# A graph-attention layer on one core: output rows made between the loop's steps instead of after the loop

## The chip, the cores and the metric

The kernel runs on one core of a Trainium2 chip. The metric is the device time of one execution in microseconds (us). Seventeen executions of the kernel before were timed; a further one was recorded by the hardware profiler, and all rows shown here are from that one.

## What is computed

12,500 nodes with 128 features, 212,500 edges sorted by their target `dst`. Cut to what matters:

```
h   = relu(layernorm(x))
q, v = h @ Wq.T + bq, h @ Wv.T + bv          # per node, 8 heads of 16
k   = edge_attr @ Wk.T + bk                  # per edge
in_m, out_m, diag_m = sum(q[src]*k), sum(q[dst]*k), sum(q[src]*q[dst])   # per edge and head
score = (softmax of each of the three over the edges of a node, summed) * edge_weight**lam
out = x + leaky_relu(segment_sum(score * v[dst]) @ Wo.T + bo)
```

Since `v[dst]` is the same for all edges of a node, a node needs from its edges only two sums for each of 24 softmaxes (3 kinds by 8 heads): the denominator and the weighted numerator.

## The kernel before

`ordered_path` relies on the order of `dst`, and sets a flag if a property that it needs does not hold. After it `general_path` runs if the flag is set; with the inputs of the reference it is not.

**Preparation.** x is loaded, the statistics `inv` and `shift` of the layer norm are taken, and q is computed and written to `q_table` in DRAM (`nodes_q`, L808 and L809), then again as three bf16 terms to `q3_table` (`terms_q`, L821 to L830). Two tables `sums` in DRAM, 48 numbers for each node, are filled with zeros from `blank` (L864, 28 DMAs on SyncE's queue, two behind each of the first `q_table` writes).

**The loop.** The edges lie in S = 5 parts that are worked in parallel, each of T = 84 blocks of 512 edges (the last block of a part is also the first of the next, but for the fifth). A *step* t takes block t of all five parts; an *iteration* g = 5 t + s takes one block. What an iteration does:

- `gather(g + 9)`: four indirect DMAs (L608), issued by GpSimd (POOL), fetch q of the sources. The ring `qq` has 11 buffers, so a gather for g + 9 waits for `logits(g - 2)`.
- `project(g + 1)`, `turn(g + 2)`, `spread_q(g + 2)`: TensorE (PE) transposes the edge features, multiplies them by Wk into `k_ps` (2 buffers), and picks q of the targets; ScalarE (ACT) copies the results.
- `logits(g)`: VectorE (DVE) multiplies q by q (L968), both by k (L969), and sums over each head (L971).
- Once a step, spread over its five iterations, the scans of the step before: `turn_logits` (s = 0), `scan_max` (s = 1, DVE), `to_rows` (PE) and `powers` (ACT) (s = 2), `scan_sums` (s = 3, DVE), `select` (s = 4, DVE). `put_rows(t - 2)` at s = 4 writes the finished sums of up to 42 nodes of each part to DRAM (L1074, 5 DMAs on SyncE's queue), at a node index that is read from the data; even parts go to one table, odd parts to the other.

The small PSUM tiles of the scans (`small`) share one ring of three buffers. The order on each engine is the program's order, which `pin` fixes: every pinned instruction comes after the one pinned before it on its engine. SyncE's queue (SP) carries `fetch_edges(g + 6)` (ring `ea` of 7), `fetch(t + 2)` at s = 3 and `put_rows`, in that order.

**The last stage.** When all sums are written, a loop over 7 chunks of 7 units (a unit is 256 nodes, 49 in all) loads the sums of both tables (`ab`) and x again, adds the tables, divides, and for every four tiles of 128 nodes: relu (L1145), transpose (L1152), copy, product with Wv (L1158), times the score (L1160), transpose (L1167), copy, product with Wo (L1173), copy, leaky relu (L1176), add x (L1178), store.

Of the kernel before, what the change touches and what calls it, by code (L numbers as in the profile page):

```python
# [7 lines left out]
F32 = mybir.dt.float32  # L8
# [8 lines left out]
HEADS = 8  # L17
# [455 lines left out]
def ordered_path(ctx: ExitStack, tc: tile.TileContext, flag, x, src, dst, edge_attr, edge_weight,  # L473
# [14 lines left out]

    nc = tc.nc
    N, F = x.shape
    E = src.shape[0]
# [16 lines left out]
    R = S * H3  # L510
    NU, CU = NI // 2, 7
    CH = 2 * CU
    LAST = N // 2 - (NU - 1) * P
    assert NI % 2 == 0 and NU % CU == 0 and N % 2 == 0 and 96 <= LAST < P

    dram = ctx.enter_context(tc.tile_pool(name="dram", bufs=1, space=DRAM))
    q_table = dram.tile([NP, F], F32, name="q_table")
    q3_table = dram.tile([3 * NP, F], BF, name="q3_table")
    rel_d = dram.tile([NB, BE], BF, name="rel_d")
    fa_d = dram.tile([NB, 4, BE], BF, name="fa_d")  # L520
    sums = [dram.tile([NP, 2 * H3], F32, name=f"sums{i}") for i in range(2)]


    consts = ctx.enter_context(tc.tile_pool(name="consts", bufs=1))
# [34 lines left out]

    inv = consts.tile([P, NI], F32, name="inv")  # L560
    shift = consts.tile([P, NI], F32, name="shift")
    blank = consts.tile([P, CU * 2 * H3], F32, name="blank")
    nc.vector.memset(blank, 0.0)
    src_i = consts.tile([P, NB, JN], I32, name="src_i")
    ends = consts.tile([P, NB, JN], F32, name="ends")
    bases = consts.tile([1, T, 8], I32, name="bases")
    tops = consts.tile([1, T, 8], I32, name="tops")
    LOOK, QQ, AHEAD, EA = 9, 11, 6, 7
    edges = ctx.enter_context(ExitStack())
    gath = edges.enter_context(tc.tile_pool(name="gath", bufs=QQ))  # L570
# [4 lines left out]
    def pin(inst):  # L575

        engine = str(inst.ins.engine)
        if engine in pinned:
            tc.add_manual_dep(inst.ins, pinned[engine], mybir.DependencyInfo(
                mybir.DependencyClass.NoSync, mybir.DependencyReason.DATA), reason="in order")  # L580
        pinned[engine] = inst.ins.name
        return inst
# [31 lines left out]
    def units(t, lo, n, c):  # L614

        return t[lo * 2 * P:(lo + n) * 2 * P, :].rearrange("(u p k) c -> p u (k c)", p=P, k=2)
# [11 lines left out]
    with tc.tile_pool(name="prep", bufs=1) as prep, \  # L628
# [14 lines left out]
        b_row = prep.tile([1, 3, F], F32, name="b_row")  # L643
        for i, b in enumerate((bv, bk, bo)):
            pin(nc.sync.dma_start(b_row[:, i, :], b[None, :]))
        nc.vector.memset(bases, 0)
        nc.vector.memset(tops, 0)
        for s in range(S):
# [204 lines left out]
        for g in range(-2, GN):  # L853
            if g + 2 < GN:
                rectify(g + 2)
            if 0 <= g + 1 < GN:
                turn_h(g + 1)
            if g >= 0:
                nodes_q(g)
            ready(g + 4)  # L860
            measure(g + 6 + min(max(g, 0), 6))
            if 0 <= g < NI // CU:
                for t in sums:
                    pin(nc.sync.dma_start(t.rearrange("(p i) r -> p (i r)", p=P)  # L864
                                          [:, g * CU * 2 * H3:(g + 1) * CU * 2 * H3], blank))
            if g in side:
                side[g]()
        for g in range(LOOK):
# [6 lines left out]
                edges_5()  # L875
        bad = got["bad"]

        found = prep.tile([1, 5], F32, name="found")
        bad_ps = prep_ps.tile([1, P], F32, name="t_ps")
        pin(nc.tensor.transpose(bad_ps[:, :RW], bad, ident[:RW, :RW]))  # L880
        nc.vector.tensor_reduce(found[:, 0:1], bad_ps[:, :RW], AX.X, ALU.min)  # L881
        nc.vector.tensor_scalar(found[:, 0:1], found[:, 0:1], 0.0, None, op0=ALU.is_lt)
        base_f = prep.tile([1, T, 8], F32, name="base_f", tag="terms")
        pin(nc.vector.tensor_copy(base_f, bases))
        top_f = tops.bitcast(F32)
        pin(nc.vector.tensor_copy(top_f, tops))
# [6 lines left out]
        nc.vector.tensor_sub(halo[:, 0:S - 2], base_f[:, 1, 2:S], base_f[:, 0, 1:S - 1])  # L893
        nc.vector.tensor_scalar(halo[:, 0:S - 2], halo[:, 0:S - 2], float(W) - 0.5, None, op0=ALU.is_lt)
        nc.vector.tensor_reduce(found[:, 3:4], halo[:, 0:S - 2], AX.X, ALU.max)
        nc.vector.tensor_reduce(found[:, 4:5], found[:, 0:4], AX.X, ALU.max)
        nc.vector.tensor_copy(flag, found[:, 4:5])


    with tc.tile_pool(name="work", bufs=2) as work, \  # L900
            tc.tile_pool(name="scan", bufs=2) as scan, \
# [76 lines left out]
        def small(shape, name):  # L978
            return ps.tile(shape, F32, name=name, tag="small", bufs=3)
# [90 lines left out]
        def put_rows(t):  # L1070
            for i, (lo, own) in enumerate(trios):
                for k in own:
                    if lo + k == 0 or t > 0:
                        pin(nc.sync.dma_start(sums[(lo + k) % 2][bass.ds(base_v[t][lo + k], W), :],  # L1074
                                              st[t]["rows"][k * W:(k + 1) * W, i, k, :]))
            del st[t], base_v[t]

        def later(f, t):
            if 0 <= t < T:
                f(t)  # L1080

        fetch(0)
        fetch(1)
# [7 lines left out]
        for g in range(end + 2 * S):  # L1091
# [25 lines left out]
            else:  # L1117
                later(select, t - 1)
                later(put_rows, t - 2)

    edges.close()


    with tc.tile_pool(name="fin", bufs=2) as fin, \
            tc.tile_pool(name="fin_ps", bufs=2, space=PSUM) as fin_ps:
        for lo in range(0, NU, CU):
            ab = fin.tile([P, 2, CH, 2 * H3], F32, name="ab", bufs=3)
            for i in range(2):
                nc.sync.dma_start(ab[:, i].rearrange("p (u k) r -> p u (k r)", k=2),
                                  units(sums[i], lo, CU, 2 * H3))  # L1130
            x_in = fin.tile([P, CH, F], F32, name="x_in", bufs=3)
            nodes_in(x_in, lo, CU, nc.sync)
            tot = fin.tile([P, CH, 2, H3], F32, name="tot")
            nc.vector.tensor_add(tot.rearrange("p n i c -> p n (i c)"), ab[:, 0], ab[:, 1])
            ratio = fin.tile([P, CH, H3], F32, name="ratio")
            nc.vector.tensor_scalar(ratio, tot[:, :, 0, :], 1e-30, None, op0=ALU.max)
            nc.vector.reciprocal(ratio, ratio)  # L1137
            nc.vector.tensor_mul(ratio, ratio, tot[:, :, 1, :])
            score = fin.tile([P, CH, HEADS], F32, name="score")
            nc.vector.tensor_add(score, ratio[:, :, 0:HEADS], ratio[:, :, HEADS:2 * HEADS])  # L1140
            nc.vector.tensor_add(score, score, ratio[:, :, 2 * HEADS:])
            h = fin.tile([P, CH, F], F32, name="h")
            for i in range(CH):
                n = 2 * lo + i
                nc.scalar.activation(h[:, i, :], x_in[:, i, :], AF.Relu, bias=shift[:, n:n + 1],  # L1145
                                     scale=inv[:, n:n + 1])
            y = fin.tile([P, CH, F], F32, name="y")
            for i in range(0, CH, JN):
                nb = min(JN, CH - i)
                h_ps = fin_ps.tile([P, JN, P], F32, name="h_ps")  # L1150
                for b in range(nb):
                    nc.tensor.transpose(h_ps[:, b, :], h[:, i + b, :], ident)  # L1152
                hT = fin.tile([P, JN, P], F32, name="hT")
                nc.scalar.copy(hT[:, :nb], h_ps[:, :nb])
                v_ps = fin_ps.tile([P, JN, F], F32, name="v_ps")
                nc.tensor.matmul(v_ps[:, :nb, :], ones3, bv3[:, :nb, :], start=True, stop=False)  # L1156
                for b in range(nb):
                    nc.tensor.matmul(v_ps[:, b, :], hT[:, b, :], wv, start=False,  # L1158
                                     stop=(b == nb - 1))
                nc.vector.tensor_mul(  # L1160
                    h[:, i:i + nb, :].rearrange("p n (h d) -> p (n h) d", d=DIM),
                    v_ps[:, :nb, :].rearrange("p n (h d) -> p (n h) d", d=DIM),
                    score[:, i:i + nb, :].rearrange("p n h -> p (n h)")[:, :, None]
                    .to_broadcast([P, nb * HEADS, DIM]))
                h_ps = fin_ps.tile([P, JN, P], F32, name="h_ps")
                for b in range(nb):
                    nc.tensor.transpose(h_ps[:, b, :], h[:, i + b, :], ident)  # L1167
                vT = fin.tile([P, JN, P], F32, name="vT")
                nc.scalar.copy(vT[:, :nb], h_ps[:, :nb])  # L1169
                o_ps = fin_ps.tile([P, JN, F], F32, name="o_ps")  # L1170
                nc.tensor.matmul(o_ps[:, :nb, :], ones3, bo3[:, :nb, :], start=True, stop=False)
                for b in range(nb):
                    nc.tensor.matmul(o_ps[:, b, :], vT[:, b, :], wo, start=False, stop=(b == nb - 1))  # L1173
                o = fin.tile([P, JN, F], F32, name="o")
                nc.scalar.copy(o[:, :nb], o_ps[:, :nb])  # L1175
                nc.vector.scalar_tensor_tensor(o[:, :nb], o[:, :nb], SLOPE, o[:, :nb], op0=ALU.mult,  # L1176
                                               op1=ALU.max)
                nc.vector.tensor_add(y[:, i:i + nb], o[:, :nb], x_in[:, i:i + nb, :])  # L1178
            y = y.rearrange("p (u k) f -> p u (k f)", k=2)
            full = min(lo + CU, NU - 1) - lo  # L1180
            nc.sync.dma_start(units(out, lo, full, F), y[:, :full, :])
            if full < CU:
                nc.sync.dma_start(out[(NU - 1) * 2 * P:, :].rearrange("(p k) f -> p (k f)", k=2),
                                  y[:LAST, full, :])


@with_exitstack
# [42 lines left out]
```

## Time and profile before

| | |
|---|---|
| median of 17 runs | 2478.63 us (2473.37 to 2488.97) |
| the profiled execution | 2479.14 us; its span on the core 2477.3 us |
| granted TensorE clock over the span | 0.807 |
| DVE, POOL, PE, ACT busy | 2138.8, 1692.4, 1748.3, 1499.0 us |

Where the stages lie in the span, by the first and last instructions of each in the timeline:

| us from the start | stage |
|---|---|
| 0 to 100.9 | statistics, q, `q_table`; the zeros of `sums` are issued from 46.0 to 81.6 |
| 100.9 to 184.8 | `q3_table`; the first 44 gathers, until `qq` is full at 161.8 |
| 184.8 to 2302.0 | the loop, to the last L971 |
| 2302.0 to 2322.0 | the scans and sums of the last two steps drain |
| 2322.0 to 2477.3 | the last stage |

A group's row reads: line, engine, operation, what it writes from what it reads, shapes, count, then the time it was busy in all and the mean of one in ns, then the idle time of its engine just before it and what ended most of that.

### The profile page before, as it was taken

The page shows a single profiled execution, that of the slowest core. Times are in us where ns is not written, and L with a number is a line of the kernel's source. Part 1 is how long each engine was busy: PE and PEld are TensorE (multiplying, and loading weights), DVE is VectorE, ACT ScalarE, POOL GpSimd, SP SyncE. Part 2 cuts the span into 40 slices and gives each one's busy share as a digit, 9 for nine tenths or more (in the row PEclk, how much of TensorE's full clock was granted, in tenths as well). Part 3 has the DMA queues.
Part 4 walks back from the last instruction along what each step waited for, and adds up shares of the span by engine and source line. Part 5 has one row for each costly group of instructions (what it writes and reads, how often), then busy time and mean ns, then how long its engine had stood idle before and what let it go on. Part 6 is the DMA issues. An engine that isn't in the chain of part 4 may idle for free. (4 is left out here: it accounts for less than half of the span.)

```text
span 2477.3 us, 35097 instructions
## 1 busy us (share of the span) xinstructions
PE 1748.3 (71%) x10635; PEld 1413.2 (57%) x10635; DVE 2138.8 (86%) x2178; ACT 1499.0 (61%) x2806; POOL 1692.4 (68%) x1714
## 2 busy tenths in 40 slices
PE   5317877777777777777777777776786767767476
PEld 4215665666565665655655566655565656656355
DVE  6559999999999999898998989999899988999563
ACT  5547666666666565666655656566565665656354
POOL 2547777777777777777777777777777777777000
PEclk8758888888878887878788877798878888878599
DMA  8755455454444544445444544444444444443532
GB/s 224 239 172 155 140 154 142 138 151 130 140 137 137 144 129 141 131 130 149 128 139 134 142 137 129 135 139 138 139 126 138 138 141 137 130 136 88 117 101 76
DMA packets 307123, 345.21 MB, mean 139 GB/s; under 512 B 134531, under 2 KB 225944, under 8 KB 306613
## 3 DMA queue, kind: packets, MB, share of 16 engines
q1 hardware_dynamic: 252474, 229.91, 30.6%
q0 software_dynamic: 54448, 112.96, 17.9%
q8 instruction: 85, 1.39, 0.2%
q14 instruction: 116, 0.95, 0.1%
HBM read 309.91 MB, written 32.76 MB: 138 GB/s over the span
## 5 line engine op out<-in xcount | busy, mean ns | idle before, releaser
L608 POOL DMA_INDIRECT qq<-q_table,src_i x1680 | 1659.4, 988 | 545.6 <-issue 427.9
L950 PEld LDWEIGHTS k_ps<-wk,eT 128*128 128x128 f32 x3360 | 521.7, 237 | 614.4 <-issue 386.8
L971 DVE TENSOR_REDUCE lT<-prod 128x96 f32<-128x1536 f32 x420 | 736.2, 1753 | 14.3
L942 ACT COPY eT<-eT_ps 128x512 f32<-128x512 f32 x420 | 245.7, 585 | 719.2 <-PE eT_ps L940 717.3
L950 PE MATMUL k_ps<-wk,eT 128*128 128x128 f32 x3360 | 617.8, 340 | 11.7 <-ACT eT L942 7.7
L969 DVE TENSOR_TENSOR prod<-qq,k_ps 128x1024 f32<-128x1024 f32 x420 | 509.9, 1214 | 2.5 <-PE k_ps L950 2.5
L948 PE MATMUL k_ps<-b,ones 3*128 3x512 bf16 x420 | 183.4, 437 | 450.1 <-DVE prod L969 449.0
L968 DVE TENSOR_TENSOR prod<-qq 128x512 f32<-128x512 f32 x420 | 286.7, 683 | 163.9 <-DMA qq<-q_table,src_i 136.3
L940 PE MATMUL eT_ps<-ident,ea 128*128 128x128 f32 x1680 | 323.6, 328 | 2.9 <-DVE found L881 2.9
L934 ACT ACTIVATE relb<-relb,before 126x512 bf16<-126x512 bf16 x420 | 308.2, 734 | 7.1 <-DMA relb<-rel_d 7.1
L935 ACT ACTIVATE oh<-relb 126x512 bf16<-126x512 bf16 x420 | 264.6, 630 | 13.4
L940 PEld LDWEIGHTS eT_ps<-ident,ea 128*128 128x128 f32 x1680 | 259.4, 174 | 3.2 <-DVE found L881 3.2
L961 ACT COPY qq<-qd_ps 128x512 f32<-128x512 f32 x420 | 248.3, 591 | 0.7 <-PE qd_ps L959 0.7
L959 PE MATMUL qd_ps<-win,oh 126*128 126x128 bf16 x1680 | 200.0, 253 | 36.6 <-ACT oh L935 30.7
L1049 PE MATMUL b_ps<-ident,sum 120*128 120x120 f32 x672 | 139.0, 338 | 87.3 <-ACT l L991 83.8
L1062 PE MATMUL w_ps<-back,sel 128*126 128x144 f32 x1344 | 198.5, 305 | 1.3 <-ACT back L1050 1.3
L959 PEld LDWEIGHTS <-oh 126*128 126x128 bf16 x1680 | 161.3, 117 | 49.7 <-ACT oh L935 32.0
L1062 PEld LDWEIGHTS w_ps<-back,sel 128*126 128x126 f32 x1344 | 185.3, 203 | 2.0 <-ACT back L1050 2.0
L1049 PEld LDWEIGHTS b_ps<-ident,sum 120*128 120x128 f32 x672 | 100.8, 214 | 135.5 <-ACT l L991 101.6
L1050 ACT COPY back<-b_ps 128x480 f32<-128x480 f32 x168 | 97.4, 580 | 46.0 <-PE b_ps L1049 46.0
L1001 DVE TENSOR_TENSOR_SCAN u<-l,u,far_ps 120x512 f32<-120x512 f32 x83 | 105.5, 1271 | 1.4 <-ACT l L991 1.4
L1029 DVE TENSOR_TENSOR_SCAN sum<-keep,sum,e 120x512 f32<-120x512 f32 x83 | 106.0, 1277 | 0.0
(155 smaller groups left out, 1666.4 us busy)
## 6 DMA issues: line engine op xcount, KB each, us to landing
ea<-in_edge_attr_dram SPq DMA_DIRECT2D x419, 256.0 KB
relb<-rel_d SPq DMA_DIRECT2D x84, 630.0 KB
qq<-q_table,src_i POOLq DMA_INDIRECT x1680
win<-q_table SPq DMA_DIRECT2D x420, 31.5 KB
q_table<-q SPq DMA_DIRECT2D x24, 384.0 KB
fa<-fa_d SPq DMA_DIRECT2D x420, 4.0 KB
sums<-rows SPq DMA_DIRECT2D x416, 7.9 KB
q_table<-xq SPq DMA_DIRECT2D x24, 256.0 KB
```

What stands on the lines that cost most here:

```text
L608: pin(nc.gpsimd.indirect_dma_start(out=qq[:, j, 0, :], out_offset=None, in_=q_table, in_offset=bass.IndirectOffsetOnAxis(ap=src_i[:, g % S ...
L934: pin(nc.scalar.activation(d, d, AF.Abs, bias=before[:K3]))
L935: pin(nc.scalar.activation(st[t]["oh"][:, s, :], d, AF.Relu, bias=1.0, scale=-1.0))
L940: pin(nc.tensor.transpose(eT_ps[:, j, :], eas[g][:, j * F:(j + 1) * F], ident))
L942: pin(nc.scalar.copy(eT, eT_ps))
L950: pin(nc.tensor.matmul(k_ps[:, j, :], eTs[g][:, j, :], wk, start=False, stop=(j == JN - 1)))
L959: pin(nc.tensor.matmul(qd_ps[:, j, :], d["oh"][:, s, j * P:(j + 1) * P], d["win"][:, s, :], start=(j == 0), stop=(j == JN - 1)))
L961: pin(nc.scalar.copy(qqs[g][:, :, 1, :], qd_ps))
L968: pin(nc.vector.tensor_mul(prod[:, :, 2, :], qqs[g][:, :, 0, :], qqs[g][:, :, 1, :]))
L969: pin(nc.vector.tensor_mul(prod[:, :, 0:2, :], qqs[g], ks[g][:, :, None, :].to_broadcast([P, JN, 2, F])))
L971: pin(nc.vector.tensor_reduce(lTs[t][:, :, s, :], prod.rearrange("p j i (h d) -> p j (i h) d", d=DIM), AX.X, ALU.add))
L1062: pin(nc.tensor.matmul(w_ps[:, i].rearrange("p s c -> p (s c)"), d["sel"][:, j, lo:lo + 3, :].rearrange("p s w -> p (s w)"), d["back"][:, ...
```

## The change

1. **A table for each part.** `sums` becomes five tables. The zeros leave the preparation: in iterations 0 to 4 ScalarE issues one DMA each that zeroes in table g the units that part g touches, from a `blank` of 96 columns. A unit is touched by one part or by two (`parts_of`).
2. **Output between the steps.** Of the 49 units 41 belong to one part and have a fixed step by which their sums are complete, from the mean rate of nodes for each step (30) and a margin of 90 nodes (`stored_at`). 40 of them are taken two at a time at an even step from 18 to 82, 20 pairs in all. In that step and the three after it `nodes_between` runs the pair's work at fixed iterations: load sums and x on SyncE's queue (s = 0), relu on ACT (s = 2 and 3), the division on DVE (s = 2); in the next step transpose (s = 1), product with Wv and multiplication by the score (s = 4); then transpose (s = 1), product with Wo, leaky relu, add (s = 4); then the store (s = 0). Their PSUM tiles come from the ring `small`.
3. **The flag.** The margin is compared with the first node of every block (`due` against `base_f`), and the result goes into the flag.
4. **The last stage** works on the nine units left (18, 9, 10, 19, 28, 29, 38, 39, 48), as five objects that pass through four stages shifted against each other. x is loaded for the first four, and relu done for the first three, in the last two steps of the drain. `x_in` has four buffers, so the fifth's x waits for the first's store.

```
-    sums = [dram.tile([NP, 2 * H3], F32, name=f"sums{i}") for i in range(2)]
+    sums = [dram.tile([NP, 2 * H3], F32, name=f"sums{i}") for i in range(S)]
...
-            if 0 <= g < NI // CU:
-                for t in sums:
-                    pin(nc.sync.dma_start(t.rearrange("(p i) r -> p (i r)", p=P)
-                                          [:, g * CU * 2 * H3:(g + 1) * CU * 2 * H3], blank))
...
+        nc.vector.tensor_sub(far, base_f, due)
+        nc.vector.tensor_reduce(found[:, 4:5], far, AX.XY, ALU.min)
+        nc.vector.tensor_scalar(found[:, 4:5], found[:, 4:5], -float(NEAR), None, op0=ALU.is_lt)
...
+        def scores(self):
+            n = self.n
+            den, num = self.ab[:, :n, 0:H3], self.ab[:, :n, H3:]
+            pin(nc.vector.tensor_scalar(den, den, 1e-30, None, op0=ALU.max))
+            pin(nc.vector.reciprocal(den, den))
+            pin(nc.vector.tensor_mul(num, num, den))
...
+        def turn(self, to):
+            for b in range(self.n):
+                pin(nc.tensor.transpose(to[:, b, :], self.h[:, b, :], ident))
+            self.hT = fin.tile([P, JN, P], F32, name="hT")
+            pin(nc.scalar.copy(self.hT[:, :self.n], to[:, :self.n]))
...
+        def project_o(self, to):
+            n = self.n
+            self.product(to, bo3, wo)
+            o, y = self.h[:, :n], self.x[:, :n]
+            pin(nc.scalar.copy(o, to[:, :n]))
+            pin(nc.vector.scalar_tensor_tensor(o, o, SLOPE, o, op0=ALU.mult, op1=ALU.max))
+            pin(nc.vector.tensor_add(y, o, y))
...
-                        pin(nc.sync.dma_start(sums[(lo + k) % 2][bass.ds(base_v[t][lo + k], W), :],
+                        pin(nc.sync.dma_start(sums[lo + k][bass.ds(base_v[t][lo + k], W), :],
...
+        def nodes_between(t, s):
+            new, old = pairs.get(t - t % 2), pairs.get(t - t % 2 - 2)
+            even = t % 2 == 0
+            if new and even and s == 0:
+                new.load_sums()
+                new.load_x()
+            if new and even and s == 2:
+                new.normalize(0, 2)
+                new.scores()
+            if new and even and s == 3:
+                new.normalize(2, 4)
+            if new and not even and s == 1:
+                new.turn(small([P, JN, P], "node_ps"))
+            if new and not even and s == 4:
+                new.project_v(small([P, JN, F], "node_ps"))
+            if old and even and s == 1:
+                old.turn(small([P, JN, P], "node_ps"))
+            if old and even and s == 4:
+                old.project_o(small([P, JN, F], "node_ps"))
+            if old and not even and s == 0:
+                old.store()
...
+            nodes_between(t, s)
+            if g < S:
+                of = [u for u in range(NU) if g in parts_of(u)]
+                pin(nc.scalar.dma_start(
+                    units(sums[g], of[0], len(of), 2 * H3),
+                    blank[:, None, :].to_broadcast([P, len(of), 2 * 2 * H3])))
...
+        for r in range(len(rest) + 3):
+            if r < len(rest):
+                if r >= 4:
+                    rest[r].load_x()
+                rest[r].load_sums()
+                if r >= 3:
+                    rest[r].normalize(0, 4)
+                rest[r].scores()
+                rest[r].turn(tile_for("h_ps"))
+            if 0 <= r - 1 < len(rest):
+                rest[r - 1].project_v(tile_for("v_ps"))
+            if 0 <= r - 2 < len(rest):
+                rest[r - 2].turn(tile_for("u_ps"))
+            if 0 <= r - 3:
+                rest[r - 3].project_o(tile_for("o_ps"))
+                rest[r - 3].store()
```

## The prediction

> **What bounds the kernel now.** I read the page's busy digits first, then the groups, then the loop's waits, then the timeline of the two ends.
>
> ```profile
> span 2477.3 us, 35097 instructions
> ...
> DVE  6559999999999999898998989999899988999563
> ...
> POOL 2547777777777777777777777777777777777000
> ...
> L608 POOL DMA_INDIRECT qq<-q_table,src_i x1680 | 1659.4, 988 | 545.6 <-issue 427.9
> ...
> L968 DVE TENSOR_TENSOR prod<-qq 128x512 f32<-128x512 f32 x420 | 286.7, 683 | 163.9 <-DMA qq<-q_table,src_i 136.3
> ```
>
> DVE with its nines looks like the bound, and POOL with its sevens does not. The groups turn this round: the idle time in front of POOL's gathers is mostly "issue", so POOL waits for nothing; and DVE's idle time lies almost all in front of L968, ended by the landing of a gather. The loop from 300 to 2250 us, by line:
>
> ```profile
> L608 POOL DMA_INDIRECT qq<-q_table,src_i x1512 | 1490.1, 985 | 460.9 <-issue 363.4 <-DVE prod L969 18.9 <-DVE prod L968 17.4
> ...
> L968 DVE TENSOR_TENSOR prod<-qq 128x512 f32<-128x512 f32 x383 | 261.4, 682 | 150.1 <-DMA qq<-q_table,src_i 133.3 <-ACT qq L961 8.0 <-ACT e L1016 5.7
> ```
>
> 1490.1 + 460.9 is the whole 1950: POOL issues gather after gather, 1512 in 1950 us, one in 1.290 us, 20 in a step, so a step takes 25.8 us. **POOL's gather pace is the loop.** DVE is busy 1784 of the 1950 us and has 166 to spare, 2.2 us a step.
>
> Then the end, which no gather hides. Columns: stretch, its length, then busy time and count of PE, PEld, DVE, ACT, POOL, then clock, DMA share, GB/s.
>
> ```profile
> 2302.00:2323.00 21.00, 15.47 (x58) 12.03 (x58) 7.02 (x8) 6.17 (x11) 0.00 (x0) 0.62 0.01 3
> 2323.00:2335.00 12.00, 0.08 (x1) 0.00 (x0) 3.74 (x4) 0.09 (x1) 0.00 (x0) 0.57 0.71 185
> 2335.00:2410.00 75.00, 56.32 (x322) 42.89 (x322) 47.44 (x75) 47.33 (x111) 0.00 (x0) 0.84 0.53 142
> 2410.00:2477.30 67.30, 47.39 (x319) 35.85 (x318) 26.13 (x48) 32.31 (x72) 0.31 (x1) 0.96 0.23 74
> ```
>
> A drain of 20 us, 12 us in which only loads run, then 142 us bound by PE's chain with its copies. The chain of waits shows its pace for each group of four tiles, 4.55 us:
>
> ```profile
> 2455.53 1.17 PE o_ps L1173 x8
> 2460.08 1.17 PE o_ps L1173 x8
> 2464.63 1.16 PE o_ps L1173 x8
> ```
>
> **The zeros leave the preparation.** DVE ends the last q (L808) at 91.0, but SP issues the last four q_table writes from 93.08 to 97.79, and only then the first six edge loads and the q3 writes:
>
> ```profile
> 93.08 4.71 SPq L809 DMA_DIRECT2D q_table<-xq  x4
> 97.84 3.00 SPq L600 DMA_DIRECT2D ea<-in_edge_attr_dram  x6
> 100.94 64.83 SPq L830 DMA_DIRECT2D q_table<-q  x25
> ```
>
> The first gather starts at 100.90. Ahead of those writes lay 28 zeroing DMAs, about 0.5 us of SP each, 4.7 MB (28 x 168 KB), at a DMA share of 0.8. Without them SP keeps up with DVE: the last write goes out about 92, the gathers and the q3 chain start some 6 us sooner, and the loop with them: **-6** (0 if the landing of the other writes decides; -8 if all of the lag goes). The five new zeroing DMAs cost ACT about 0.5 us each (SP's price for such an issue) in a loop where ACT is busy 1218 of 1950 us: 0.
>
> **The test of the margin.** Five small DVE operations more, on 420 elements instead of 672 (L887 with 672: 0.85 us), end before DVE's wait of 10.68 us for ACT at 179.67: 0. POOL's `iota` ahead of the loads of src: 0.3 to 0.6 us, 0 if the loads hide it. Base minus due lies between -14 and 20 over the reference's inputs, the margin is 90: the flag stays off.
>
> **The loop, DVE.** For a pair (four tiles): L1160, L1176 and L1178 at 0.69, 0.69, 0.68; reciprocal of 96 elements, from 2.25 us for 336 (L1137), about 0.7; maximum, product and two additions from L1136, L1138 and L1140, 0.17, 0.2, 0.17, 0.17. Together 3.5 us, 69 us for 20 pairs (the other way: all DVE work of the last stage, 83 us, times 40/49 is 68). From step 18 on DVE has 67 x 2.2 = 147 us of idle time. Pairs come every 2 to 4 steps, so the load is 0.9 to 1.75 us a step against 2.2 free, and the 11 buffers let POOL run on while DVE is behind. **0**; uncovered it would be +69.
>
> **The loop, other engines.** ACT: 4 x 0.485 (L1145) + 3 x 0.585 = 3.7 us a pair. PE: about 4.5 us a pair, in a loop where it is busy 1441 of 1950. SP: six DMAs a pair. The loads wait for the last put to land (1.3 us each in the drain), behind them stand edge loads that are six iterations ahead; the store waits for DVE's addition of the iteration before, about 8 us of SP, and behind it again edge loads with 10 us to spare; `fetch` waits for PE anyway (513 us in SP's waits). The five puts no longer wait for each other (162 us in SP's waits, none of it on the path). **0.**
>
> **POOL itself.** Here a rule speaks against the change. A gather alone takes 0.944 us (median), the mean is 0.988. The long ones stand where DVE runs L968:
>
> ```profile
> 1017.55 0.69 DVE L968 TENSOR_TENSOR prod<-qq 128x512 f32<-128x512 f32 x1
> 1017.69 1.36 POOL L608 DMA_INDIRECT qq<-q_table,src_i  x1 [0.30 <-issue]
> ```
>
> Counted over the trace: of the gathers that start inside an L968 (two inputs in SBUF) 73% are stretched, 60 us in all, 0.143 us for each of the 420 L968, 0.21 us for each us of it; of the gathers that start inside L969, L971 or the scans, which have one SBUF input, none is. The Trainium skill ("SBUF — State Buffer", Who interferes with whom) says that a DVE instruction with two SBUF inputs contends with a GpSimd instruction that reads SBUF, and that the later one blocks until the first ends. The pairs add such instructions: leaky relu, addition, product, two score additions, 1.9 us a pair, 38 us in all. By the rule with every one hit, POOL loses up to 38 us; by the row's share 38 x 0.21 = **+8**, which I take, since most gathers start in other DVE time; 0 to +38. Here a POOL delay is a loop delay.
>
> **The drain.** The last pair's transposes stand on PE in front of `to_rows`: about 1.6 us cold (4 x 0.4, as at 2335.46), and one more user of the ring of three makes the last `b_ps` wait for the second scan, 1.2 us; the three serial puts of 1.3 us give some back: **+2** (0 to +5).
>
> **The last stage**, counted from 2322.0. Puts 2.0, three loads and landing 3.5: 5.5. Division of objects 0 and 1 (one waits for its loads), score product: 9.9. Object 2's division, product 1, two transposes: 13.4. Product with Wo, copy, leaky relu, addition, store: 17.8. Object 4's x waits for that store: landing 2, load 2.2, relu 1: 23.5 at its transpose, and PE's order holds all behind it. Then PE's rounds, 5, 4.5, 3 and 1 us, and copy, leaky relu, addition, store: 38.6. From the last store's issue (2470.1) to the span's end it is 7.2 us now: 46. So 155.3 becomes about 45: **-110** (-116 to -100). Its clock starts low (0.57 to 0.62 in these rows), which is in the estimate's 1.1 us for a transpose and 2 us for a product.
>
> **Sum**: -6 + 0 + 8 + 2 - 110 = -106. Against the profiled execution's 2479.1 that is **2373 us**; that execution is 0.5 us over the median of 17, so nothing is corrected. Of the terms' ends: 2479 - 124 = 2355 to 2479 - 57 = 2422.
>
> **Rivals.**
> - *DVE becomes the bound* and its 69 us come on top, 2373 + 69 = 2442 (half of it: 2407). For: 86% busy, lines of nines. Against: its idle time ends with gathers. 12%.
> - *The ring of three holds PE* (the slower side). A pair's transpose takes the buffer of `far_ps`, so PE stands until `scan_max` is done: L971 and the scan after the k_ps release, 1.75 + 1.27 = 3.0 us, and k for the next blocks is late by that and the transpose. By the timeline k is needed 7.7 us after the release and would come at 6.3 to 7, so it is hidden. If each of the 80 uses cost DVE 3.0 us, 240 less the 78 us that DVE has left is +162: 2535. It turns the sign above (106 + 78) / 80 = 2.3 us a use. 8%.
> - *The flag is set.* Then `general_path` runs too, with 3322 gathers at 1.29 us, over 6600 us. The inputs exclude it: 1%.
> - The forecast: 79%.
>
> A difference under 0.2% (5 us) can't be told from none. Faster: the forecast and the first rival, less a little for partial cases of the second, 0.89; same 0.02; slower 0.09. The range 2352 to 2422 leaves out half of the first rival, the other two, and some 5% of the forecast.
>
> **What would show it.** Right: POOL's gathers follow each other through the loop with no idle time but issue; DVE's idle time before L968 falls from 164 to about 95 us; the last L971 comes within 10 us of 2302; 45 us from the last `rows` copy to the end. Wrong: POOL waiting for DVE (L971) in the loop; gathers with a mean over 1.0 us; PE waiting for `scan_max` in front of a pair's transpose while DVE then waits for `k_ps`; a last stage over 60 us.

## The result, and the profile after

The changed kernel takes **2371.93 us** (median of 8 runs, 2370.43 to 2375.5) where the kernel before takes 2479.25 us in its 47 runs beside it. The ratio is 0.9565, with a 95% interval of 0.9553 to 0.9578. The profiled execution took 2371.0 us, with a span of 2368.9 us at a granted clock of 0.814. The forecast was 2373 us.

The page of the changed kernel, its span, busy digits and two groups (the gather is L625 here, the first product L1092):

```profile
span 2368.9 us, 35159 instructions
...
DVE  7559999998999999999999999999999999999983
...
POOL 3547777777777777777777777777777777777750
...
L625 POOL DMA_INDIRECT qq<-q_table,src_i x1680 | 1661.9, 989 | 547.2 <-issue 422.2
...
L1092 DVE TENSOR_TENSOR prod<-qq 128x512 f32<-128x512 f32 x420 | 286.3, 682 | 98.0 <-DMA qq<-q_table,src_i 80.7
```

DVE's nines now run through to the end, and POOL's row is what it was. The gather's mean went from 988 to 989 ns. DVE's idle time in front of the first product fell from 163.9 to 98.0 us, and most of it still ends with a gather. The same two groups from 300 to 2250 us, and three that the pairs have brought in:

```profile
L625 POOL DMA_INDIRECT qq<-q_table,src_i x1511 | 1490.4, 986 | 460.6 <-issue 355.4 <-ACT relb L1058 14.3 <-DVE prod L1093 14.0
...
L1092 DVE TENSOR_TENSOR prod<-qq 128x512 f32<-128x512 f32 x382 | 260.4, 682 | 87.1 <-DMA qq<-q_table,src_i 80.5 <-ACT eT L1066 4.1 <-ACT qq L1085 1.0
...
L973 DVE RECIPROCAL ab<-ab 128x96 f32<-128x96 f32 x19 | 14.3, 753 | 0.7
L993 DVE TENSOR_TENSOR h<-node_ps,score 128x512 f32<-128x512 f32 x19 | 13.0, 683 | 0.0
L1005 DVE TENSOR_TENSOR x_in<-h,x_in 128x512 f32<-128x512 f32 x18 | 12.5, 692 | 0.6
```

1490.4 + 460.6 is 1951 us again: POOL is never without a gather in hand. No idle time between two gathers of the loop exceeds 0.4 us, in either kernel. Where the 108.4 us between the two spans lie, from one execution of each:

| stage | before | after | difference | predicted |
|---|---|---|---|---|
| up to the first gather of the loop proper (the 45th) | 184.8 | 176.5 | -8.3 | -6 |
| from it to the last gather | 2109.1 | 2112.2 | +3.1 | +8 |
| last gather to the last sum over heads | 8.2 | 8.4 | +0.2 | 0 |
| drain, to the last `rows` copy | 19.9 | 19.5 | -0.4 | +2 |
| last stage | 155.3 | 52.3 | -103.0 | -110 |

The stretches of the end (columns as before: stretch, length, busy time and count of PE, PEld, DVE, ACT, POOL, then clock, DMA share, GB/s):

```profile
2297.00:2316.60 19.60, 14.75 (x67) 11.81 (x67) 8.87 (x11) 8.82 (x18) 0.00 (x0) 0.67 0.18 56
2316.60:2337.00 20.40, 16.71 (x60) 11.97 (x60) 9.41 (x29) 7.56 (x18) 0.00 (x0) 0.51 0.20 50
2337.00:2347.60 10.60, 0.03 (x1) 0.03 (x1) 1.82 (x4) 1.40 (x4) 0.31 (x1) 0.64 0.13 41
2347.60:2368.90 21.30, 11.85 (x58) 8.57 (x58) 6.71 (x14) 4.25 (x9) 0.00 (x0) 0.74 0.14 46
```

The third row stands out: 10.6 us in which PE does nothing. The timeline shows what it waits for:

```profile
2339.30 0.82 SPq L1011 DMA_DIRECT2D out_dram<-x_in  x2
2342.16 0.31 POOL L931 MEMSET x_in<- 32x256 f32 x1 [52.51 <-DMA out_dram<-x_in]
2342.49 0.27 SPq L932 DMA_DIRECT2D x_in<-in_x_dram  x1
2347.02 0.88 ACT L966 ACTIVATE h<-x_in,shift,inv 128x128 f32<-128x128 f32 x2 [9.20 <-DMA x_in<-in_x_dram]
2347.57 0.86 PE L981 MATMUL h_ps<-ident,h 128*128 128x128 f32 x2 [10.91 <-ACT h L966]
```

The first object's store has to land before the fifth object's x may be loaded into its buffer. The store goes out at 2339.30, the buffer is cleared at 2342.16, x lands at 2347.0, and PE's transposes, behind which the others' work is queued, stand 10.91 us. Why the first store comes so late is seen a little earlier, in the order of PE's work before the product with Wo (`o_ps`) that it needs:

```profile
2329.10 1.63 PE L981 MATMUL h_ps<-ident,h 128*128 128x128 f32 x4 [1.12 <-ACT h L966]
2331.19 2.08 PE L988 MATMUL v_ps<-wv,hT 128*128 128x128 f32 x8
2333.06 1.06 PE L981 MATMUL u_ps<-ident,h 128*128 128x128 f32 x4
2334.58 2.08 PE L988 MATMUL o_ps<-wo,hT 128*128 128x128 f32 x8
```

The first three are the fourth object's transposes, the third object's product with Wv and the second object's transposes.

### The profile page after: what moved, and what is told of

It is laid out like the page before. It is cut to its first block, busy times and chain, and to the rows that moved or that the text cites. A ratio compares the mean times of both kernels' runs of the same rounds, so it can differ in the third digit from the quotient of the medians.

```text
span 2368.9 us, 35159 instructions
## 1 busy us (share of the span) xinstructions
PE 1728.6 (73%) x10629; PEld 1395.5 (59%) x10629; DVE 2146.9 (91%) x2263; ACT 1490.3 (63%) x2797; POOL 1696.6 (72%) x1715
## 5 line engine op out<-in xcount | busy, mean ns | idle before, releaser
L625 POOL DMA_INDIRECT qq<-q_table,src_i x1680 | 1661.9, 989 | 547.2 <-issue 422.2
L1074 PE MATMUL k_ps<-wk,eT 128*128 128x128 f32 x3360 | 619.1, 341 | 20.1 <-ACT eT L1066 16.6
L1093 DVE TENSOR_TENSOR prod<-qq,k_ps 128x1024 f32<-128x1024 f32 x420 | 509.9, 1214 | 2.5 <-PE k_ps L1074 2.5
L1092 DVE TENSOR_TENSOR prod<-qq 128x512 f32<-128x512 f32 x420 | 286.3, 682 | 98.0 <-DMA qq<-q_table,src_i 80.7
L1059 ACT ACTIVATE oh<-relb 126x512 bf16<-126x512 bf16 x420 | 264.5, 630 | 13.4
L1186 PE MATMUL w_ps<-back,sel 128*126 128x144 f32 x1344 | 186.9, 293 | 0.6 <-ACT back L1174 0.6
L1186 PEld LDWEIGHTS w_ps<-back,sel 128*126 128x126 f32 x1344 | 173.2, 192 | 1.0 <-ACT back L1174 1.0
```

What stands on the lines that cost most here:

```text
L625: pin(nc.gpsimd.indirect_dma_start(out=qq[:, j, 0, :], out_offset=None, in_=q_table, in_offset=bass.IndirectOffsetOnAxis(ap=src_i[:, g % S ...
L1059: pin(nc.scalar.activation(st[t]["oh"][:, s, :], d, AF.Relu, bias=1.0, scale=-1.0))
L1074: pin(nc.tensor.matmul(k_ps[:, j, :], eTs[g][:, j, :], wk, start=False, stop=(j == JN - 1)))
L1092: pin(nc.vector.tensor_mul(prod[:, :, 2, :], qqs[g][:, :, 0, :], qqs[g][:, :, 1, :]))
L1093: pin(nc.vector.tensor_mul(prod[:, :, 0:2, :], qqs[g], ks[g][:, :, None, :].to_broadcast([P, JN, 2, F])))
L1186: pin(nc.tensor.matmul(w_ps[:, i].rearrange("p s c -> p (s c)"), d["sel"][:, j, lo:lo + 3, :].rearrange("p s w -> p (s w)"), d["back"][:, ...
```

## The experiments

Three questions were open. What in the preparation gave 8.3 us, the zeros' bytes or their issues on SyncE? What do the pairs cost in the loop, and why less than the rule and the row said? What of the last stage's gain is due to placing work in the loop, and what is left in it? All times are beside runs of the kernel before at 2478.78 to 2479.76 us, but for one pair of runs that is named.

### The zeros: bytes or issues

*Five zeroing DMAs back in the preparation*, on SyncE's queue instead of ScalarE's in the loop:

```
+            if 0 <= g < S:
+                of = [u for u in range(NU) if g in parts_of(u)]
+                pin(nc.sync.dma_start(units(sums[g], of[0], len(of), 2 * H3), blank[...]))
```

> The changed kernel with its five zeroing DMAs (2.6 MB) issued by SyncE behind the first five q_table writes of the preparation, not by ScalarE in the loop. Theory A, the gain at the loop's start (first gather 9.7 us sooner, first loop gather 8.3 us sooner) came from SyncE's issue time of 28 DMAs: five of them cost 1 to 2 us, 2373 us. Theory B, it came from the 4.7 MB that lay ahead of the q_table writes in the DMA engines: 2.6 of 4.7 MB give back 4 to 5 us, 2376.5 us; the first gather near 96.

Measured: 2371.85 us (ratio 0.9568, 0.9552 to 0.9584); first gather at 90.3 us, against 91.4 in the changed kernel. The 2.6 MB and their five issues cost nothing that can be seen there.

*28 zeroing DMAs more*, two behind each of the first `q_table` writes as in the kernel before, of the old size into two spare tables (4.7 MB), and of 24 columns each (0.34 MB):

```
+            if 0 <= g < NI // CU:
+                for t in spare:
+                    pin(nc.sync.dma_start(t[...][:, g * CU * 2 * H3:...], wide[:, :CU * 2 * H3]))   # or wide[:, :24]
```

> The changed kernel plus the 28 zeroing DMAs of before at their old places (4.7 MB, into two spare tables that nothing reads). Both theories: the whole gain is given back, first loop gather 8 us later, 2380 us. If less than 4 us comes back, the gain had another cause than the zeros.

> As the run with 28 spare zeroing DMAs, but each writes only 24 of its 336 columns (as many DMAs and rows, 0.34 MB instead of 4.7 MB). Theory A (issue time of SyncE): 7 to 8 us come back, 2379.5 us. Theory B (bytes in the DMA engines): at most 1 to 2 us, 2373 us.

Measured: 2374.88 us (0.957 to 0.9596) with the full size, 2374.7 us (0.9565 to 0.9591) with the small one. The first gather comes at 97.7 and 97.9 us, the loop proper at 181.6 and 182.1, that is 5.1 and 5.6 us later than in the changed kernel. SyncE's queue in the changed kernel, and then in the one with 28 small DMAs:

```profile
83.59 4.49 SPq L829 DMA_DIRECT2D q_table<-xq  x4
88.13 3.00 SPq L617 DMA_DIRECT2D ea<-in_edge_attr_dram  x6
```

```profile
90.06 4.72 SPq L832 DMA_DIRECT2D q_table<-xq  x4
94.83 3.00 SPq L618 DMA_DIRECT2D ea<-in_edge_attr_dram  x6
```

The last q on DVE, which these writes store, in the kernel before, the changed one and the one with 28 small DMAs:

```profile
89.97 1.02 DVE L808 TENSOR_TENSOR xq<-q_ps,bq_all 128x512 f32<-128x512 f32 x2 [0.56 <-PE q_ps L805]
```

```profile
85.90 1.02 DVE L828 TENSOR_TENSOR xq<-q_ps,bq_all 128x512 f32<-128x512 f32 x2 [0.56 <-PE q_ps L825]
```

```profile
87.64 1.02 DVE L831 TENSOR_TENSOR xq<-q_ps,bq_all 128x512 f32<-128x512 f32 x2 [0.56 <-PE q_ps L828]
```

So the start of the first gather has three parts: the end of the last q on DVE, the lag of SyncE's last table write behind it, and some 3 us more.

| us | last q ends | lag of the last write | first gather |
|---|---|---|---|
| before | 91.0 | 6.8 | 100.9 |
| after | 86.9 | 1.2 | 91.4 |
| 28 full DMAs more | 88.5 | 6.1 | 97.7 |
| 28 small DMAs more | 88.7 | 6.1 | 97.9 |

Eight traces leave the 28 DMAs out with the rest of this preparation unchanged: the changed kernel, the one with five DMAs back, and six of the kernels below. In them the lag is 0.7 to 1.9 us. The 28 DMAs bring it back to 6.1, with a fourteenth of the bytes as with all of them: it is the count of issues, some 5 us, and not the bytes. The other part of the gain is not of the zeros. The last q ends 4.1 us sooner, and in the eight traces anywhere from 86.7 to 90.0; the fourth q already starts at 43.8 us in the kernel before and at 40.1 in the changed one, ahead of the first zeroing DMA at 46.0. In the seven of these traces that also leave the five DMAs out of the preparation, the loop proper starts between 176.5 and 179.8 us. The profiled execution of the changed kernel is the earliest of them, so its 8.3 us are the upper end of 5.0 to 8.3 against the one execution of the kernel before.

The whole time rose by 2.9 us where 8 were expected; by the time alone, the sign of another cause that was named ahead (less than 4 us back) would be met. But the intervals of the ratios overlap with the changed kernel's, and in the five traces that have the changed loop, from the 45th gather to the last, it takes 2109.4 to 2114.3 us: the total can't tell a few microseconds, the queue can.

### What the loop is bound by

*A quarter of the gathers made plain.* One of an iteration's four indirect DMAs becomes a plain load of 128 consecutive rows of the same table on SyncE's queue. This kernel leaves out a quarter of the sources' rows and takes other nodes' rows in their place:

```
-            for j in range(JN):
+            pin(nc.sync.dma_start(qq[:, JN - 1, 0, :], q_table[g % NI * P:(g % NI + 1) * P, :]))
+            for j in range(JN - 1):
```

> The changed kernel with three of the four gathers of an iteration; the fourth quarter of qq is filled by one plain DMA of SyncE's queue with 128 consecutive rows (so a quarter of the source rows are other nodes' rows). My account: POOL needs 19.4 us a step then, and DVE becomes the bound with 23.4 us a step plus the pairs' 69 us, a loop of about 2040 instead of 2117 us: 2295 us. Rival, the landing of the rows or another queue sets the pace and POOL only follows: 2350 us or more.

Measured: 2286.38 us (ratio 0.9223, 0.9201 to 0.9245). The groups of its loop from 300 to 2250 us:

```profile
L626 POOL DMA_INDIRECT qq<-q_table,src_i x1148 | 1197.0, 1043 | 661.0 <-issue 348.9 <-DVE lT L1096 48.5 <-ACT oh L1060 48.2
...
L1093 DVE TENSOR_TENSOR prod<-qq 128x512 f32<-128x512 f32 x393 | 267.3, 680 | 0.4 <-ACT up L1137 0.4
```

Now POOL waits and DVE doesn't: 0.4 us of idle time in front of the first product. From the first gather of the loop proper (the 34th here, three for each of 11 buffers before it) to the last sum over heads it is 2033.6 us, against 2120.6 in the changed kernel. That is DVE's own pace with all 20 pairs in it, 87 us under POOL's. The first rival (DVE the bound) is out for the kernel as it is.

### What an operation of DVE costs POOL

*One more DVE operation a step*, of the pairs' commonest shape (128 x 512), behind the second product, 84 in all; once with one input in SBUF and one in PSUM (it writes a product again that is there), once with both inputs in SBUF:

```
+            if s == 2:
+                pin(nc.vector.tensor_mul(prod[:, :, 0, :], qqs[g][:, :, 0, :], ks[g]))
```

```
+            if s == 2:
+                pin(nc.vector.tensor_mul(prod[:, :, 2, :], qqs[g][:, :, 0, :], qqs[g][:, :, 1, :]))
```

> The changed kernel plus one DVE product of 128x512 a step with one input in SBUF and one in PSUM (84 in all, 0.68 us each, 57 us; its result is overwritten with the same values). My account (POOL is the loop, DVE has some 98 us of idle time left): 2372 us, at most 3 us more, DVE's idle time before the first product falls by about 50 us. Rival, DVE is by now the bound: 2410 to 2429 us.

> As the run with one more DVE product a step, at the same place and of the same size, but with both inputs in SBUF. By the row of before (0.143 us of gather stretch for each such product): 84 x 0.143 = 12 us, 2384 us, mean gather 0.995 us. By the rule that the later instruction blocks for the whole of the other, with every one hit: up to 57 us, 2429 us. If the inputs don't matter: 2372 us, as the other run.

Measured: 2403.4 us (ratio 0.9698, 0.9673 to 0.9723) and 2399.79 us (0.9678, 0.9657 to 0.97). The first missed by 31 us, the second by 16. The first comes near its rival's 2410, but DVE is not the bound in either: POOL has no gap over 0.4 us, and from 300 to 2250 us DVE still idles 56.9 and 66.4 us in front of the first product. What grew are the gathers themselves. A stretch of the timeline with the two-input operation (L1096) shows how:

```profile
1015.29 0.69 DVE L1092 TENSOR_TENSOR prod<-qq 128x512 f32<-128x512 f32 x1
1015.43 1.37 POOL L625 DMA_INDIRECT qq<-q_table,src_i  x1 [0.31 <-issue]
1015.89 1.21 DVE L1093 TENSOR_TENSOR prod<-qq,k_ps 128x1024 f32<-128x1024 f32 x1
1017.02 0.69 DVE L1096 TENSOR_TENSOR prod<-qq 128x512 f32<-128x512 f32 x1
1017.10 1.43 POOL L625 DMA_INDIRECT qq<-q_table,src_i  x1 [0.31 <-issue]
1017.74 1.75 DVE L1097 TENSOR_REDUCE lT<-prod 128x96 f32<-128x1536 f32 x1
1018.83 0.94 POOL L625 DMA_INDIRECT qq<-q_table,src_i  x1 [0.30 <-ACT e L1142]
```

The gather at 1015.43 starts 0.14 us into L1092 and takes 0.43 us more than the usual 0.944. L1092 had 0.55 us left by its record. The next starts 0.08 us into L1096 and takes 0.49 more; 0.61 were left. Over all stretched gathers of these traces the extra time is what the record leaves, less 0.13 us in the mean of each operation, from 0.69 to 1.02 us long. So the gather stands until the operation ends. Of the gathers that start with 0.3 us or more of such an operation left, 25 in seven traces are not stretched, all of them in its first 0.05 us. And then POOL lies at a fixed distance behind DVE: the next gather starts 1.12 us after the recorded end (0.944 and the 0.305 between two gathers, less the 0.13), and L1093 fills all but the last 0.08 us of that. The two engines don't drift past each other; a blocked gather sets the time of those that follow.

Summing what gathers of the loop take over 0.944 us (those of 0.99 and more), by the DVE operation that each ran into:

| us | first product | select (L1162) | difference (L1128) | the pairs' | the added one | sum |
|---|---|---|---|---|---|---|
| before | 59.7 | 6.0 | 1.8 | - | - | 68 |
| after | 59.4 | 7.0 | 2.8 | 1.5 | - | 71 |
| one input more | 85.9 | 8.9 | 1.3 | 1.9 | 0 | 98 |
| two inputs more | 54.6 | 7.3 | 1.8 | 2.4 | 35.9 | 102 |

The two-input operation blocks 76 gathers in 84 executions, at 0.09 us from its start in the mean: nearly its full length each time, 35.9 us. For 70 of the 76 the gather before was one that the first product had held. The one-input operation blocks none of the 15 gathers that start in it. But it moves DVE against POOL, so that 245 gathers instead of 181 run into the first product: 26.5 us. The loops' growth from the 45th gather to the last (27.1 and 31.1 us) is the growth of these sums (27.3 and 31.3). The expectation for one input failed because it held the hits on the first product fixed.

### The last stage

*The fifth object's x and relu ahead of the last stage*, in buffers of its own:

```
-            self.x = fin.tile([P, JN, F], F32, name="x_in", bufs=4)
+            self.x = (fin.tile([P, JN, F], F32, name="x_in", bufs=4) if self.n > 2
+                      else fin.tile([P, 2, F], F32, name="x_last", bufs=1))
...
-                for r in rest[s:min(s + 1, 4)]:
+                for r in (rest[s:s + 1] if s < 3 else rest[3:] if s == 3 else []):
...
-                if r >= 4:
-                    rest[r].load_x()
```

(`h` in the same way; the added table's buffer `more` becomes smaller to make room.)

> The changed kernel with tiles of their own for x and relu of the fifth object of the last stage, loaded with the others in the drain, so that it no longer waits for the first object's store. My account of the last stage: PE's idle time of 10.9 us in front of that object's transposes goes, the rest stays, 2362 us (last stage 42 to 43 us instead of 52.3). Rival, PE's low clock and the chain over DVE bound the last stage and the wait is only where it shows: a gain under 3 us, 2369 us or more.

Measured: 2364.28 us (ratio 0.954, 0.9527 to 0.9553), 7.7 us under the changed kernel. The fifth object's transposes in its timeline:

```profile
2338.35 0.86 PE L984 MATMUL h_ps<-ident,h_last 128*128 128x128 f32 x2 [1.61 <-ACT h_last L969]
```

The wait is 1.61 us instead of 10.91, and the time is 7.7 us less. The rival (a gain under 3 us) is out. But the last stage is not the expected 42 to 43 us in this trace: it takes 47.3 us (2315.25 to 2362.5), since from these transposes to the end it is 24.2 us, at a granted clock of 0.58, where the changed kernel has 21.3 at 0.74. In the trace of the kernel that joins this change with another, further below, it is 20.1 us at 0.77, and the stage 43.1 us. The seven traces with the old wait have stages of 49.9 to 54.2 us, so a single trace of this stage is good to some 2 us.

*No pairs.* All 49 units are left to the new last stage, as 25 objects, with x for the first four ahead and eight buffers for the rest; the loop runs without `nodes_between`:

```
-    for t in range(0, T - 1, 2):
+    for t in range(0, 0, 2):
...
+        for r in rest[:4]:
+            r.load_x()
...
-                if r >= 4:
-                    rest[r].load_x()
+                if r + 4 < len(rest):
+                    rest[r + 4].load_x()
```

> The changed kernel without any pair in the loop: all 49 units go as 25 objects through the new last stage (x four objects ahead, in eight buffers; x and relu start after the drain). My account: the place of the work in the loop's free time is what gains, the new last stage by itself little: 20 us to fill, 25 objects at PE's 4.6 us, 7 us behind the last store, about 145 us where the changed kernel has 52, 2463 us. Rival, the four shifted stages of the new last stage save most: last stage under 110 us, 2430 us or less.

Measured: 2573.14 us (ratio 1.0377, 1.035 to 1.0405), 110 us over the expectation. From the last sum over heads to the end it takes 276 us. A stretch of it, and the wait that sets its rounds:

```profile
2336.00:2440.00 104.00, 71.93 (x270) 48.91 (x269) 34.66 (x77) 33.65 (x71) 0.00 (x0) 0.66 0.20 60
```

```profile
2454.42 1.65 ACT L965 ACTIVATE h<-x_in,shift,inv 128x128 f32<-128x128 f32 x4 [1.48 <-DVE x_in L1004]
2454.96 1.63 PE L980 MATMUL h_ps<-ident,h 128*128 128x128 f32 x4 [3.19 <-ACT h L965]
...
2464.66 1.65 ACT L965 ACTIVATE h<-x_in,shift,inv 128x128 f32<-128x128 f32 x4 [1.49 <-DVE x_in L1004]
```

A round takes 10.2 us: relu of an object waits for the leaky relu and addition of the object four before it (four buffers of `h`), PE waits for relu, and the clock that PE is granted stays at 0.66, where the old last stage had 0.84 to 0.96. So the new stage, with its four buffers of `h`, is slower for each tile than the old one; with more buffers it was not tried. The gain does not come from the stage's form but from the 40 units' leaving it. The loop without pairs takes 2110.7 us from the 45th gather to the last, within the 2109.4 to 2114.3 us of the loops with them. DVE's idle time in front of the first product is 153.8 us from 300 to 2250 (87.1 with pairs), and its gathers' sum as in the table above is 69 us.

### A version that beats both

*The first product takes q of the targets from PSUM*, so that it has one input in SBUF; two buffers of `qd_ps`, paid for by one of `eT_ps`. Then the same with the fifth object ahead.

```
-            qd_ps = ps.tile([P, JN, F], F32, name="qd_ps")
+            qd_ps = qds[g] = ps.tile([P, JN, F], F32, name="qd_ps", bufs=2)
...
-            pin(nc.vector.tensor_mul(prod[:, :, 2, :], qqs[g][:, :, 0, :], qqs[g][:, :, 1, :]))
+            pin(nc.vector.tensor_mul(prod[:, :, 2, :], qqs[g][:, :, 0, :], qds.pop(g)))
```

> The changed kernel with the first DVE product of an iteration (L1092) reading the targets' q from PSUM (qd_ps, two buffers; eT_ps one) instead of ACT's copy in SBUF, so that it has one SBUF input. If the gathers' stretch is the lock of the instructions with two SBUF inputs, the 57 us that lie in gathers that start inside L1092 go: mean gather near 0.953 us, POOL's loop about 2055 us, still above DVE's own 2020 us that the run with three gathers gave: 2317 us. Rival, the stretch only follows the phase of POOL and DVE and other instructions take it over, or PE is held by qd_ps: 2350 us or more.

> The two together: q from PSUM and tiles of their own for the fifth object of the last stage. If they are independent, 2317 - 8 = 2309 us.

This first pair ran on a chip on which the kernel before took 3270 us at the time, and its loop was bound by something else there: in the first kernel's trace 163 of POOL's gaps exceed 0.4 us. So its times (3083.99 and 3062.41 us, ratios 0.9433 and 0.9381) don't answer the expectations. The same two kernels beside 2479.76 us:

> The loop's first product takes q of the targets from PSUM, so it has one input in SBUF instead of two (two buffers of qd_ps, paid for by one of eT_ps); the copy to SBUF stays for the table that the other products need. Theory (gathers are stretched by what is left of a two-input DVE operation that began before them): the 57 us of stretch that lie in L1092 go, the mean gather falls from 0.987 to about 0.955, and the time to about 2317 us where before takes 2479. Rival (PE waits for the one eT_ps buffer, or the product waits for PE, and DVE becomes late): no gap closes, POOL shows gaps above 0.4 us, 2350 us or more.

> The same together with x and relu of the fifth object ahead of the last stage: a further 8 us less by the last object's wait (about 2309 us where before takes 2479). If the last stage's clock eats the gain, 2317.

Measured: **2346.69 us** (ratio 0.9464, 0.9447 to 0.9481) and **2336.78 us** (0.9423, 0.9404 to 0.9443): 25 and 35 us under the changed kernel, 30 and 28 us short of the expectations. The loop of the first from 300 to 2250 us:

```profile
L625 POOL DMA_INDIRECT qq<-q_table,src_i x1532 | 1483.6, 968 | 467.1 <-issue 368.0 <-DMA qq<-q_table,src_i 19.2 <-DVE lT L1095 12.5
...
L1092 DVE TENSOR_TENSOR prod<-qq,qd_ps 128x512 f32<-128x512 f32 x388 | 262.4, 676 | 57.6 <-DMA qq<-q_table,src_i 52.9 <-ACT l L1115 3.1 <-ACT oh L1059 0.8
```

The rival that PE holds the product back is out: POOL has no gap over 0.4 us. Of the 186 gathers that start in the first product none is stretched, and its 59.4 us are gone. But the rival first named, that other operations take the stretch over, came half true: the sum over all gathers only falls from 71 to 40 us, since others now run into the operations that have kept two inputs, select from 7.0 to 26.4 us, the difference from 2.8 to 11.3. The timeline shows three of those operations in a row:

```profile
1023.78 1.02 DVE L1162 TENSOR_TENSOR sel<-ends,places 128x840 f32<-128x840 f32 x1
1024.38 1.23 POOL L625 DMA_INDIRECT qq<-q_table,src_i  x1 [0.30 <-issue]
1024.72 0.68 DVE L1004 SCALAR_TENSOR_TENSOR h<-h 128x512 f32<-128x512 f32 x1
1025.44 0.69 DVE L1005 TENSOR_TENSOR x_in<-h,x_in 128x512 f32<-128x512 f32 x1
1025.92 1.03 POOL L625 DMA_INDIRECT qq<-q_table,src_i  x1 [0.30 <-issue]
```

The first gather is held until select ends, and that places the next one 1.12 us later: past all of L1004, and in the last 0.21 us of L1005, for 0.09 us.

## Why the prediction held, term by term

The sum was -106, the spans differ by 108.4. Four terms were off by 2 to 7 us in both directions, so it is in part luck that the total came out within 3 us.

- **The bound.** "POOL's gather pace is the loop" is shown: with fewer gathers the loop runs 87 us faster, at DVE's pace.
- **The zeros, -6.** Measured -9.5 at the first gather and -8.3 at the loop's start. The mechanism as put there, SyncE's lag of 28 issues, is shown: the lag fell by 5.6 us, and 28 DMAs bring 4.9 of it back, with few bytes or many. The rest is a last q that ended 4.1 us sooner on DVE, which the prediction did not have and which scatters by 3.3 us between traces. ScalarE's price for the five was put at nothing; the kernel with them on SyncE is no different.
- **The loop on DVE, 0.** Right. The pair's operations measure 753 ns (reciprocal), 683, 686 and 692 ns (the three of 128 x 512), 0.19 to 0.26 us for the small ones: 3.7 us a pair for the 3.5 put down. Idle time in front of the first product took it up: 163.9 to 98.0, predicted about 95.
- **POOL, +8.** The mechanism was right, its size not. The Trainium skill ("SBUF — State Buffer", Who interferes with whom) says that the later of the two blocks until the first ends; the trace agrees to 0.13 us. What failed was the step "by the row's share 38 x 0.21 = **+8**", which takes gathers to start anywhere in DVE's time. They don't: of the pairs' operations L1005 alone is hit, 19 times in 20, for 0.08 us each, 1.5 us in all. Each time the gather before it had started in select, which comes just ahead of L1004 and L1005, and 18 of these were held till select ended; so the next one falls in the last 0.2 us of L1005 and never in L1004. The loop grew by 3.1 us, as the sum over all gathers did (67.6 to 70.7), but that is within the scatter of this stretch. The upper bound, 38, was no mere form: in another place 84 operations of that kind, 57 us of them, cost 36.
- **The drain, +2.** Measured -0.4. The pair's transposes take 1.1 us and wait 0.45 us for the scan of maxima. The further wait of 1.2 us of the last `b_ps` for the second scan did not come: it starts 0.15 us after that scan's end, and 0.06 us after it in the kernel before.
- **The last stage, -110.** Measured -103.0: 52.3 us for "about 45" (the prediction's own steps end at 46). The step that failed is "Object 2's division, product 1, two transposes: 13.4", after which the first object's product with Wo was to run. Up to the score product the steps are right, 10.2 for 9.9. Then PE's order puts before the product with Wo the fourth object's transposes, at the pace of its relu on ScalarE, which is not done ahead as the first three objects' is (in the drain's last step), and the third object's product with Wv, 2.6 us with its bias; the product with Wo starts at 17.5, and the first store goes out at 22.7 (2339.30 less 2316.6) instead of 17.8. Landing, load and relu of the fifth object then take 8.3 instead of 5.7, and its transposes are at 31.0 instead of 23.5. From there the 21.3 us to the end are near the 22.5 that were put. With this wait taken out the time is 7.7 us less.
- **The rivals.** DVE as the bound and the ring of three are excluded by POOL's unbroken gathers and by DVE's idle time, which ends with gathers, not with `k_ps`. The flag's path did not run.

## What to carry to other kernels

Where one engine's unbroken issues set a loop, work of other engines goes into it nearly free, here 40 units that took most of 155 us at the end; the new form of the stage, with all the work left at the end, was slower than the old form. What such work costs is not its own duration but what it does to the bounding engine, and that is read from the bounding engine's long instructions and what each of them ran into. Count issues on a queue as well as bytes, compare a stage over several traces before a difference of a few microseconds is given a cause, and let the last object of a pipeline have its inputs before the pipeline starts.

## What the runs showed of the hardware

- A gather that starts while DVE runs an operation with two SBUF inputs takes longer by what is left of that operation's record, less 0.13 us. With one of the first product's inputs in PSUM, none of the 186 gathers that start in it is stretched; with both in SBUF it was 181 of 221, most of the others in the operation's last 0.15 us. Scans and sums over heads stretch none.
- The block re-aligns POOL to DVE. So the hits are not spread evenly: one operation was hit 76 times in 84 at nearly its full length, the same kind elsewhere 19 times in 20 but for 0.08 us each, and an added operation that blocks nothing itself cost 26.5 us by moving others. Taking the two-input form from the most frequent operation gave 30 of the 59 us that were charged to it.
- 28 further DMAs on SyncE left its last table write 6.1 us behind DVE where it had been 0.7 to 1.9 us behind, a net 0.2 us each, whether each moved 12 kB or 168 kB.
